# A gated FFN beside a state-space convolution on one core: the convolution as eight block products, a split product in the first two units, one block of LoRA products for the second weight pair, and a last product in two halves

## The chip, the cores and the metric

The kernel runs on one core of a Trainium2 chip. The metric is the device time of one execution in microseconds (us). Five engines work side by side, each with its own instruction queue: TensorE (PE; its weight loads are listed apart as PEld), VectorE (DVE), ScalarE (ACT), GpSimd (POOL) and SyncE (SP), which here only issues DMAs. Matrix products end in PSUM, in banks of 128 rows by 512 f32 columns; the other engines read them from there.

## The reference

The input x has 2 x 1024 tokens of 512 features. Everything is f32. Cut to what is computed:

```python
xn = layernorm(x)                       # over the 512 features, no scale
# s: a state-space (S4) layer along the 512 features of a token
K = s4_kernel(Lambda, p, q, B, Ct, step, 512)   # Cauchy sums at 512 roots of unity, inverse FFT, real part
s = causal_conv(xn, K) + D * xn                  # by FFTs of length 1024, first 512 kept
# g: a SwiGLU FFN with LoRA (rank 16, scale 2) on each of its three weights
h1 = xn @ w1.T + 2 * (xn @ A1.T) @ B1.T          # 512 -> 1376
h3 = xn @ w3.T + 2 * (xn @ A3.T) @ B3.T          # 512 -> 1376
g0 = silu(h1) * h3
g = silu(g0 @ w2.T + 2 * (g0 @ A2.T) @ B2.T)     # 1376 -> 512
out = x + s * g
```

The convolution along 512 features is a product with a 512 x 512 triangular Toeplitz matrix. In blocks of 128 it has only four different blocks, K0 (on the diagonal, with D added) to K3. With a token's features in four blocks X0 to X3, the result has the blocks

Y0 = X0 K0, Y1 = X0 K1 + X1 K0, Y2 = X0 K2 + X1 K1 + X2 K0, Y3 = X0 K3 + X1 K2 + X2 K1 + X3 K0.

## The kernel before

**First stage, to about 270 us.** Features lie on partitions, tokens on columns. The 2048 tokens are four blocks of 512. The products with w1 and w3 are done by two nested levels of a Strassen-Winograd scheme (seven products in place of eight at each level). The hidden features are cut into five pairs of chunks and a last one of 96 rows. A *chain* (`Chain`, `add_chain`) is one sequence of seven inner products; `product` (L745, matmul at L750) issues the matmuls of one, into the banks called x, y, w and aux, of which there are two each. ACT copies bank x when a partial sum is to be kept (`snapshot`, L770), while the next product goes on accumulating into the same bank; DVE adds bank y to the copy (L774). Work that belongs between the matmuls is placed by hand: `at(place, what)` puts a call at a place on a time line counted in products (seven to a chain), `after(delay, what)` at so many places behind the present one.

The LoRA part is merged into the weights before they are used. `lora_product` (matmul at L381) multiplies the two rank-16 factors, which lie in 16 of 128 partitions, and `merge` (DVE, L391) adds the product out of PSUM to the weight tile. There are four groups of partitions (0, 32, 64, 96), and products on different groups run side by side on PE. Factors are loaded by `load_lora` into one group, for a range of hidden features: the first `LSPLIT` of them or the rest, `LSPLIT` to `HID`; the rest belongs to the last chunk and the first pairs, and is in use first. Before the change groups 0 and 1 get the rest at the start (on ACT's queue), groups 2 and 3 the first `LSPLIT` (on SP's queue), and `other_factors` later loads the first `LSPLIT` into groups 0 and 1 too. So the second pair, which needs the rest, has two groups: `merge_pair` does four products on them for one half of the features, at place 5.7, and again for the other half at 8.9. The later pairs have four groups, and `merge_whole_pair` does all eight products at once, into banks y, w and two aux.

The gated hidden values g go out to DRAM (`store_g`, L802, on SP's queue).

**Second stage, 270 us to the end.** The product with w2 is done in eight *units* of 256 tokens (128 from each of two blocks), again by seven products P1 to P7 of one Strassen-Winograd level, in half banks of 256 columns. `unit` (L1293) is a generator, and `run` steps two units, or one alone, in turn; after each step it takes one entry from a list of `parts` and, from step `s4_from` on, `s4_steps` entries from `s4_work`. The parts are mostly the group sums of the next group's g (`group_piece`, DVE, L1158: sums of blocks of a g chunk loaded by `load_g`, L1147). `s4_work` is a generator that computes the convolution's matrix on DVE, with a few matmuls: the resolvent (PE L595, DVE L613 to L627), a product at L639, the roots (DVE L648 to L673), then z, the scaled DFT tables (DVE L688 and L690, eight of each), which PE multiplies at L709, and the matrix itself in `conv`, 128 x 640 (`s4_matrix`, from L695).

The first four units only make g for their tokens and set it aside in DRAM (`set_aside`, L1277), since the matrix isn't there yet. The last four (`HOLD` = 4) do the convolution for their own tokens and for those of one unit that was set aside (`held`), which makes 16 products of 128 tokens each, `conv_product` (L915, matmuls at L922). `result` (L1284) adds what is missing in the convolution (L1288), multiplies it by the gate (L1289), adds x (L1290, on POOL, the last one on DVE) and writes the output. `silu` is L1249; L1326 and L1340 are the additions in a unit that free banks w and y.

In units 0 and 1 (`wait=True`) P1 is done without its last chunk first, and then, a step later, its last chunk, whose g comes in latest by DMA; P2 comes after both.

Before the change a convolution takes seven matmuls, two of them with 256 columns:

```python
m = (X0 + X1) K2                       # into bank w, copied by ACT
y[:, 0:256]   = X0 [K0 K1]
y[:, 256:512] = X2 [K0 K1]             # blocks 2 and 3
y[:, 384:512] += X0 K3'                # K3' = K3 - K2
y[:, 128:256] += X1 K0
y[:, 256:384] += X1 K12                # K12 = K1 - K2
y[:, 384:512] += X3 K0
y[:, 256:512] += [m m]                 # by DVE, L1288
```

The token sums X0 + X1 (`token_sums`, L1418, two DVE operations of 128 x 1024) stand at the head of the parts of units 2 and 3, behind two empty entries and ahead of the group sums of the next group.

The last unit's last product, P3, goes into one half bank of 256 columns and accumulates onto z4's source (bank x, which holds the earlier products); silu, the gate, x and the write follow for 256 columns at once.

Of the kernel before, what the change touches and what calls it, by code (L numbers as in the profile page):

```python
# [12 lines left out]
F32 = mybir.dt.float32  # L13
# [94 lines left out]
def s4_gated_ffn(  # L108
# [308 lines left out]
    def merge_whole_pair(c, w):  # L417

        ps = [[bank("y", True), bank("w", True)], [bank("aux"), bank("aux")]]
# [7 lines left out]
        for (k, v), when in zip(((0, 0), (0, 1), (1, 0), (1, 1)), (1.15, 2.3, 4.3, 4.4)):  # L427
            to = w[:, (slice(1, 3), slice(0, 4, 3))[v], k].rearrange("p s m h -> p s (m h)")
            from_ = ps[k][v].rearrange("p (s n) -> p s n", s=2)
            after(when, lambda to=to, from_=from_: merge(to, from_))  # L430
# [201 lines left out]
    def s4_roots():  # L632
# [50 lines left out]
        for lc in range(NDC):  # L683
            e_r, e_i = edft[:, 0, lc, :], edft[:, 1, lc, :]
            a_r, a_i = ar[:, lc : lc + 1], ai[:, lc : lc + 1]
            for i, (f, g, o) in enumerate(((a_i, a_r, add), (a_r, a_i, sub))):
                tz = s4_tile([P, P], "tz")
# [7 lines left out]
    def s4_matrix():  # L695
# [42 lines left out]
        k1, k2, k3, k12 = (conv[:, n * P : (n + 1) * P] for n in range(1, 5))  # L738
        nc.vector.tensor_tensor(k12, k1, k2, sub)
        yield  # L740
        nc.vector.tensor_tensor(k3, k3, k2, sub)
# [173 lines left out]
    def conv_product(lhs, x01, sb, tok, tag):  # L915

        y, m_ps = bank(tag), bank("w")[:, :P]
        x0, x1, x2, x3 = (lhs[i][:, sb, k, tok] for i in range(2) for k in range(2))
        k = [conv[:, n * P : (n + 1) * P] for n in range(5)]

        def mul(to, x_, by, start=False):
            nc.tensor.matmul(  # L922
                to, lhsT=x_, rhs=by, start=start, stop=True, skip_group_check=True
            )

        mul(m_ps, x01[:, sb, tok], k[2], True)
        m = work.tile([P, P], F32, tag="m", name="m", bufs=3)
        nc.scalar.copy(m, m_ps)
        mul(y[:, : 2 * P], x0, conv[:, : 2 * P], True)
        mul(y[:, 2 * P :], x2, conv[:, : 2 * P])  # L930
        mul(y[:, 3 * P :], x0, k[3])
        mul(y[:, P : 2 * P], x1, k[0])
        mul(y[:, 2 * P : 3 * P], x1, k[4])
        mul(y[:, 3 * P :], x3, k[0])
        return y, m
# [29 lines left out]
    for v, f in enumerate(factors):  # L965
        load_lora(nc.sync, 2 + v, *f, 0, LSPLIT)

    def other_factors():
        for v, (_, h) in enumerate(factors):
            load_lora(nc.sync, v, None, h, 0, LSPLIT)  # L970
# [113 lines left out]
    for c in range(NPAIR):  # L1084
# [7 lines left out]
        if c + 1 < NPAIR:  # L1092
# [8 lines left out]
            if c == 0:  # L1101
                for half in range(2):
                    at(5.7 + 3.2 * half, step(merge_pair, half))
# [147 lines left out]
    class Place:  # L1251
# [21 lines left out]
        def conv(self, h, tag):  # L1273
            return conv_product(lhs[h], x01[h], self.sb, self.tok, tag)
# [9 lines left out]
        def result(self, h, y, cols=slice(0, DIM), last=False):  # L1284
            o, (y, m) = self.o[h][:, cols], y
            if cols.stop == DIM:
                late = y[:, HALF:].rearrange("p (n t) -> p n t", n=2)
                nc.vector.tensor_tensor(late, late, m.unsqueeze(1).broadcast_to([P, 2, P]), add)  # L1288
# [4 lines left out]
    def unit(u, read, held=None, wait=False):  # L1293
# [21 lines left out]
        if wait:  # L1315
            pairs = [t[:, c, cut] for t in a11 for c in range(t.shape[1])]
            pairs = list(zip(pairs, b11))
            product(xb, pairs[:-1], True)
            yield
            product(xb, pairs[-1:], False)  # L1320
# [4 lines left out]
        mul(wb, a12, b21, True, [(gl[:, 0, cut], wl0)])  # L1325
# [17 lines left out]
        if last:  # L1343
# [9 lines left out]
            mul(*p3)  # L1353
            pl.result(1, y[1], lo)
            silu(o0[:, hi], xb)
            pl.result(0, y[0], hi, True)
# [50 lines left out]
    for part in (*s3, *s2):  # L1407
# [4 lines left out]
    run([unit(u, read, wait=True) for u in range(2)], [*t[:2], *s1, *s4_, *t[2:], *more], 4, 5)  # L1412
# [3 lines left out]
    x01 = [work.tile([P, NSB, TB], F32, name=f"x01_{h}", bufs=1) for h in range(2)]  # L1416
    token_sums = [
        lambda h=h: nc.vector.tensor_tensor(  # L1418
            x01[h], lhs[h][0][:, :, 0, :], lhs[h][0][:, :, 1, :], add
        )  # L1420
        for h in range(2)
    ]
# [10 lines left out]
    nothing = [lambda: None]  # L1433
# [97 lines left out]
```

## Time and profile before

| | us |
|---|---|
| median of 3 runs | 447.9 |
| fastest and slowest run | 447.69, 448.11 |
| the profiled execution, its own time | 447.56 |
| its span (first to last instruction) | 445.8 |

The TensorE clock granted in the profiled execution is full speed (1.0) in every slice. Of the 40 slices of the span (11.1 us each), PE is 90% busy or more in all but the first and the last; DVE is at 80% or more from 11 to 89 us, at 30 to 80% with single slices above it until 279 us, at 70 to 100% from there to 334 us, and at 10 to 50% from then on. ACT is busy 137.4 us in all, POOL 202.2.

A line of a timeline is: start in us, length in us, engine, line of the code, operation, output <- inputs, form, number of records (x2 means two records of the same kind one behind another; an f32 matmul leaves more than one record). In square brackets stands the idle time of the engine just before, and what ended it. Matmuls overlap, so the pitch from one start to the next is what a matmul costs, not its length. A line of DMA issues is: output <- input, queue, number, size, microseconds from issue to landing. In the list of waits a line is: engine and line that waited, what for; total, times, longest.

### The profile page before, as it was taken

The page shows a single profiled execution, that of the slowest core. Times are in us where ns is not written, and L with a number is a line of the kernel's source. Part 1 is how long each engine was busy: PE and PEld are TensorE (multiplying, and loading weights), DVE is VectorE, ACT ScalarE, POOL GpSimd, SP SyncE. Part 2 cuts the span into 40 slices and gives each one's busy share as a digit, 9 for nine tenths or more (in the row PEclk, how much of TensorE's full clock was granted, in tenths as well). Part 3 has the DMA queues.
Part 4 walks back from the last instruction along what each step waited for, and adds up shares of the span by engine and source line. Part 5 has one row for each costly group of instructions (what it writes and reads, how often), then busy time and mean ns, then how long its engine had stood idle before and what let it go on. Part 6 is the DMA issues. An engine that isn't in the chain of part 4 may idle for free.

```text
span 445.8 us, 5022 instructions
## 1 busy us (share of the span) xinstructions
PE 438.9 (98%) x1678; PEld 272.2 (61%) x1678; DVE 292.0 (66%) x496; ACT 137.4 (31%) x279; POOL 202.2 (45%) x156
## 2 busy tenths in 40 slices
PE   8999999999999999999999999999999999999996
PEld 8635334344444444444443446888898999989995
DVE  5898999946874687368836887979892214541222
ACT  2776342453245334433443242111102101011110
POOL 1315169895679548944894379200000213221221
PEclk9999999999999999999999999999999999999999
DMA  8911304025002400340054536486803742323211
GB/s 263 361 53 46 118 0 147 24 73 165 25 24 97 140 24 24 112 145 24 24 184 147 165 126 199 143 308 205 330 1 114 282 136 76 120 96 94 94 49 47
DMA packets 35257, 53.52 MB, mean 120 GB/s; under 512 B 4640, under 2 KB 21344, under 8 KB 35104
## 3 DMA queue, kind: packets, MB, share of 16 engines
q1 hardware_dynamic: 35104, 53.07, 36.2%
q8 instruction: 13, 0.21, 0.2%
q10 hardware_dynamic: 128, 0.14, 0.1%
q14 instruction: 12, 0.10, 0.1%
HBM read 33.80 MB, written 19.40 MB: 119 GB/s over the span
## 4 chain that ended last, share of the span: by engine, by line
PE 93%; DMA 2%; DVE 1%; issue 1%; POOL 1%; ACT 0%; POOLq 0%; DVEq 0%; SPq 0%
PE x L750 44%; PE y L750 23%; PE w L750 12%; PE aux L922 6%; PE w L975 2%; DMA room<-g_dram 1%; PE aux L303 1%; PE aux L381 1%; PE y L381 1%; PE w L922 1%; PE y L527 1%; PE aux L709 1%; DMA g_dram<-s 0%; POOL s L831 0%; DVE t_in L1200 0%
## 5 line engine op out<-in xcount | busy, mean ns | idle before, releaser
L1290 POOL TENSOR_TENSOR o<-o,xin 128x512 f32<-128x512 f32 (+1 forms) x17 | 22.5, 1324 | 136.9 <-DVE o L1289 136.9
L831 POOL TENSOR_TENSOR s<-c,s 128x512 f32<-128x512 f32 (+1 forms) x44 | 63.6, 1451 | 16.6 <-ACT c L823 11.5
L770 ACT COPY s<-x 128x512 f32<-128x512 f32 (+1 forms) x54 | 31.6, 586 | 87.8 <-PE x L750 86.5
L750 PE MATMUL x<-t_in,s 128*128 128x512 f32 (+1 forms) x148 | 55.2, 500 | 0.0
L774 DVE TENSOR_TENSOR s<-s,y 128x512 f32<-128x512 f32 (+1 forms) x54 | 36.1, 680 | 17.1 <-PE y L750 10.9
L864 POOL TENSOR_TENSOR s<-ua_three,s 128x512 f32<-128x512 f32 x20 | 32.4, 1619 | 26.9 <-DVE s L774 26.9
L750 PEld LDWEIGHTS x<-t_in,s 128*128 128x128 f32 x148 | 26.8, 190 | 22.8 <-issue 12.5
L864 POOL TENSOR_TENSOR ua_three<-ua_three,s 128x512 f32<-128x512 f32 x20 | 33.0, 1650 | 13.6 <-DVE s L774 13.6
L750 PE MATMUL y<-t_in,s 128*128 128x256 f32 (+1 forms) x108 | 35.9, 459 | 0.0
L1312 ACT COPY z<-x 128x256 f32<-128x256 f32 x24 | 8.8, 372 | 79.9 <-PE x L750 79.9
L864 POOL TENSOR_TENSOR s<-u_three,s 128x512 f32<-128x512 f32 x20 | 28.5, 1425 | 1.8 <-ACT c L823 1.0
L823 ACT ACTIVATE c<-c 128x512 f32<-128x512 f32 x40 | 25.2, 632 | 8.8 <-DVE c L864 8.8
L750 PEld LDWEIGHTS y<-t_in,s 128*128 128x128 f32 x108 | 20.1, 190 | 11.5 <-issue 8.8
L788 ACT COPY w<-x 128x512 f32<-128x512 f32 (+1 forms) x37 | 21.1, 570 | 12.2 <-PE x L750 12.1
L922 PE MATMUL aux<-conv,xr 128*128 128x128 f32 (+1 forms) x128 | 23.2, 314 | 0.0
L1288 DVE TENSOR_TENSOR aux<-aux,m 128x256 f32<-128x256 f32 x16 | 6.9, 431 | 23.1 <-PE aux L922 23.1
L864 POOL TENSOR_TENSOR u_three<-ua_three,u_three 128x512 f32<-128x512 f32 x10 | 12.7, 1272 | 18.3 <-DVE u_three L774 18.3
L750 PE MATMUL x<-t_in,w 128*128 128x512 f32 x40 | 20.8, 603 | 0.0
L750 PE MATMUL x<-xr,w 128*128 128x512 f32 x40 | 20.6, 614 | 0.0
L750 PE MATMUL x<-xt,w 128*128 128x512 f32 x40 | 20.6, 597 | 0.0
L750 PE MATMUL x<-xr,s 128*128 128x512 f32 x40 | 20.5, 613 | 0.0
L750 PE MATMUL x<-xt,s 128*128 128x512 f32 x40 | 20.4, 592 | 0.0
(282 smaller groups left out, 877.2 us busy)
## 6 DMA issues: line engine op xcount, KB each, us to landing
g_dram<-s SPq DMA_DIRECT2D x40, 256.0 KB, 2.1
g<-g_dram SPq DMA_DIRECT2D x10, 512.0 KB, 5.8
xin<-in_x_dram SPq DMA_DIRECT2D x16, 256.0 KB, 2.7
out_dram<-o SPq DMA_DIRECT2D x14, 256.0 KB, 2.0
t_in<-g_dram SPq DMA_DIRECT2D x6, 512.0 KB, 4.2
w<-in_w1T_dram SPq DMA_DIRECT2D x10, 256.0 KB, 4.4
w<-in_w3T_dram SPq DMA_DIRECT2D x10, 256.0 KB, 3.9
s<-in_x_dram SPq DMA_DIRECT2D x8, 256.0 KB, 4.3
```

Source lines behind the costliest of these rows:

```text
L381: nc.tensor.matmul(ps, lhsT=d[:, dc * P : (dc + 1) * P], rhs=h, start=start, stop=True, skip_group_check=True,)
L750: nc.tensor.matmul(ps[:, cols], lhsT=lhsT, rhs=rhs if parts == 1 else rhs[:, cols], start=first and i == 0 and part == 0, stop=i == len(pa ...
L770: nc.scalar.copy(t, self.x)
L774: nc.vector.tensor_tensor(t, t, self.y, add)
L788: nc.scalar.copy(self.w, self.x)
L823: nc.scalar.activation(c, c if src is None else src, AF.Silu)
L831: nc.gpsimd.tensor_tensor(g, act, g, mult)
L864: (nc.vector if o < 20 else nc.gpsimd).tensor_tensor(to, a, b, add)
L922: nc.tensor.matmul(to, lhsT=x_, rhs=by, start=start, stop=True, skip_group_check=True)
L975: nc.tensor.matmul(ps[:, i % 4 * P : (i % 4 + 1) * P], lhsT=ident, rhs=ident, start=first and i == 0, stop=True, skip_group_check=True,)
L1290: (nc.vector if last else nc.gpsimd).tensor_tensor(o, o, self.xin[h][:, cols], add)
L1312: nc.scalar.copy(t, xb)
```

## The change

It has four parts.

1. **Convolution.** Eight products of 128 columns replace the seven. A bank w now gets X1 (K0 + K2), X0 (K1 + K2) and X2 (K0 + K1), side by side. ACT copies these 384 columns into a tile m, and the first 128 of them once more behind. Bank y gets X0 K0, X0 K3, (X0 + X1) (-K2) into block 1, (X1 - X2 - X0) K1 into block 2 and (X3 - X2 - X1) K0 onto block 3. DVE then adds m's columns 0 to 384, and then its columns 128 to 512, to y's blocks 1 to 3, one 128 x 384 addition each. The token sums are made in 128 x 512 operations, five for each of four pairs of tokens and super-block (`block_sums`): those of the first super-block are appended to `s4_work`, the others are entries in the parts of unit `HOLD`. The two old token sums leave the parts of units 2 and 3. X3 is overwritten by its sum; the other sums lie in tiles that are free by then. The matrix part makes K0 + K2, K1 + K2, K0 + K1 and -K2 in place of K12 and K3'.
2. **Units 0 and 1.** The steps are now P1 without its last chunk, P2 without its last chunk, P1's last, P2's last. Two empty entries go into the parts behind the first two, and `s4_from` goes from 5 to 7.
3. **LoRA of the second pair.** `merge_whole_pair` at place 5.7 takes the place of the two `merge_pair`. It is given two banks w in place of y and w, and its own delays for the four merges. For this groups 2 and 3 are loaded with the rest of the factors, `LSPLIT` to `HID` (608 columns), and `other_factors` loads the first `LSPLIT` into all four groups: four DMAs where there were two.
4. **The last unit's P3.** It is done in two halves of 128 columns. The first goes into another bank x, from zero, and DVE adds z4 to it; the second accumulates as before. Each half is followed by its own silu, gate, addition of x and write.

```diff
@@ -414,9 +414,9 @@
...
-    def merge_whole_pair(c, w):
-        ps = [[bank("y", True), bank("w", True)], [bank("aux"), bank("aux")]]
+    def merge_whole_pair(c, w, first=None, delays=(1.15, 2.3, 4.3, 4.4)):
+        ps = [first or [bank("y", True), bank("w", True)], [bank("aux"), bank("aux")]]
         for half in range(2):
...
@@ -424,7 +424,7 @@
...
                     )
-        for (k, v), when in zip(((0, 0), (0, 1), (1, 0), (1, 1)), (1.15, 2.3, 4.3, 4.4)):
+        for (k, v), when in zip(((0, 0), (0, 1), (1, 0), (1, 1)), delays):
             to = w[:, (slice(1, 3), slice(0, 4, 3))[v], k].rearrange("p s m h -> p s (m h)")
...
@@ -684,7 +684,7 @@
...
             for i, (f, g, o) in enumerate(((a_i, a_r, add), (a_r, a_i, sub))):
-                tz = s4_tile([P, P], "tz")
+                tz = conv[:, DIM:]
                 nc.vector.tensor_scalar(tz, e_i, f, None, mul)
...
@@ -735,10 +735,14 @@
...
         yield
-        k1, k2, k3, k12 = (conv[:, n * P : (n + 1) * P] for n in range(1, 5))
-        nc.vector.tensor_tensor(k12, k1, k2, sub)
-        yield
-        nc.vector.tensor_tensor(k3, k3, k2, sub)
+        k0, k1, k2, _, k01 = (conv[:, n * P : (n + 1) * P] for n in range(5))
+        k2s = s4["k2s"]
+        both = conv[:, : 2 * P].rearrange("p (n t) -> p n t", n=2)
+        nc.vector.tensor_tensor(k2s, both, k2.unsqueeze(1).broadcast_to([P, 2, P]), add)
+        yield
+        nc.vector.tensor_tensor(k01, k0, k1, add)
+        yield
+        nc.vector.tensor_scalar(k2, k2, -1.0, None, mult)
         yield
...
@@ -912,27 +916,36 @@
...
-    def conv_product(lhs, x01, sb, tok, tag):
-        y, m_ps = bank(tag), bank("w")[:, :P]
-        x0, x1, x2, x3 = (lhs[i][:, sb, k, tok] for i in range(2) for k in range(2))
-        k = [conv[:, n * P : (n + 1) * P] for n in range(5)]
-        def mul(to, x_, by, start=False):
+    def conv_product(lhs, x01, x12, sb, tok, tag):
+        y, shared = bank(tag), bank("w")
+        x0, x1, x2, x321 = (lhs[i][:, sb, k, tok] for i in range(2) for k in range(2))
+        k0, k1, k2, k3, k01 = (conv[:, n * P : (n + 1) * P] for n in range(5))
+        def mul(to, n, x_, by, start=False):
             nc.tensor.matmul(
-                to, lhsT=x_, rhs=by, start=start, stop=True, skip_group_check=True
+                to[:, n * P : (n + 1) * P],
+                lhsT=x_,
+                rhs=by,
+                start=start,
+                stop=True,
+                skip_group_check=True,
             )
-        mul(m_ps, x01[:, sb, tok], k[2], True)
-        m = work.tile([P, P], F32, tag="m", name="m", bufs=3)
-        nc.scalar.copy(m, m_ps)
-        mul(y[:, : 2 * P], x0, conv[:, : 2 * P], True)
-        mul(y[:, 2 * P :], x2, conv[:, : 2 * P])
-        mul(y[:, 3 * P :], x0, k[3])
-        mul(y[:, P : 2 * P], x1, k[0])
-        mul(y[:, 2 * P : 3 * P], x1, k[4])
-        mul(y[:, 3 * P :], x3, k[0])
-        return y, m
+        mul(shared, 0, x1, s4["k2s"][:, 0], True)
+        mul(shared, 1, x0, s4["k2s"][:, 1])
+        mul(shared, 2, x2, k01)
+        m = work.tile([P, DIM], F32, tag="m", name="m", bufs=2)
+        nc.scalar.copy(m[:, : 3 * P], shared[:, : 3 * P])
+        nc.scalar.copy(m[:, 3 * P :], shared[:, :P])
+        mul(y, 0, x0, k0, True)
+        mul(y, 3, x0, k3)
+        mul(y, 1, x01[sb][:, tok], k2)
+        mul(y, 2, x12[sb][:, tok], k1)
+        mul(y, 3, x321, k0)
+        return [y, m, True]
...
@@ -963,11 +976,12 @@
...
     for v, f in enumerate(factors):
-        load_lora(nc.sync, 2 + v, *f, 0, LSPLIT)
+        load_lora(nc.sync, 2 + v, *f, LSPLIT, HID)
...
         for v, (_, h) in enumerate(factors):
-            load_lora(nc.sync, v, None, h, 0, LSPLIT)
+            for group in (v, 2 + v):
+                load_lora(nc.sync, group, None, h, 0, LSPLIT)
...
@@ -1099,8 +1113,12 @@
...
             if c == 0:
-                for half in range(2):
-                    at(5.7 + 3.2 * half, step(merge_pair, half))
+                at(
+                    5.7,
+                    lambda nx=nx: merge_whole_pair(
+                        nx, w_pair[nx], [bank("w"), bank("w")], (1.6, 2.6, 4.8, 5.8)
+                    ),
+                )
             else:
...
@@ -1271,7 +1289,7 @@
...
         def conv(self, h, tag):
-            return conv_product(lhs[h], x01[h], self.sb, self.tok, tag)
+            return conv_product(lhs[h], x01[h], x12[h], self.sb, self.tok, tag)
...
@@ -1282,10 +1300,12 @@
...
         def result(self, h, y, cols=slice(0, DIM), last=False):
-            o, (y, m) = self.o[h][:, cols], y
-            if cols.stop == DIM:
-                late = y[:, HALF:].rearrange("p (n t) -> p n t", n=2)
-                nc.vector.tensor_tensor(late, late, m.unsqueeze(1).broadcast_to([P, 2, P]), add)
+            o, made = self.o[h][:, cols], y
+            y, m, parts = made
+            if parts:
+                for n in range(2):
+                    nc.vector.tensor_tensor(y[:, P:], y[:, P:], m[:, n * P : (n + 3) * P], add)
+                made[2] = False
             nc.vector.tensor_tensor(o, o, y[:, cols], mult)
...
@@ -1313,16 +1333,23 @@
...
         if wait:
-            pairs = [t[:, c, cut] for t in a11 for c in range(t.shape[1])]
-            pairs = list(zip(pairs, b11))
-            product(xb, pairs[:-1], True)
+            one, two = (
+                list(zip([t[:, c, cut] for t in a for c in range(t.shape[1])], b))
+                for a, b in ((a11, b11), (a12, b21))
+            )
+            product(xb, one[:-1], True)
             yield
-            product(xb, pairs[-1:], False)
+            product(wb, two[:-1] + [(gl[:, 0, cut], wl0)], True)
+            yield
+            product(xb, one[-1:], False)
         else:
...
         yield
-        mul(wb, a12, b21, True, [(gl[:, 0, cut], wl0)])
+        if wait:
+            product(wb, two[-1:], False)
+        else:
+            mul(wb, a12, b21, True, [(gl[:, 0, cut], wl0)])
         nc.vector.tensor_tensor(o0[:, lo], z1, wb, add)
...
@@ -1350,10 +1377,19 @@
...
             yield
-            mul(*p3)
-            pl.result(1, y[1], lo)
-            silu(o0[:, hi], xb)
-            pl.result(0, y[0], hi, True)
+            other = bank("x")[:, :P]
+            chunks = [t[:, c, cut] for t in s4_ for c in range(t.shape[1])]
+            for n, to in enumerate((other, xb[:, P:])):
+                part = slice(n * P, (n + 1) * P)
+                cols = slice(HALF + n * P, HALF + (n + 1) * P)
+                pairs = [(a, b[:, part]) for a, b in (*zip(chunks, b22), (gl[:, 0, cut], wl1))]
+                product(to, pairs, n == 0)
+                if n == 0:
+                    pl.result(1, y[1], lo)
+                    nc.vector.tensor_tensor(o0[:, cols], z4[:, part], to, add)
+                silu(o0[:, cols], to if n else o0[:, cols])
+                pl.result(0, y[0], cols, True)
             return
...
@@ -1409,17 +1445,41 @@
...
     after_, more = following(1)
-    run([unit(u, read, wait=True) for u in range(2)], [*t[:2], *s1, *s4_, *t[2:], *more], 4, 5)
+    nothing = [lambda: None]
+    run([unit(u, read, wait=True) for u in range(2)], [*t[:2], *nothing * 2, *s1, *s4_, *t[2:], *more], 4, 7)
...
     lhs = [[xr[:, 0], xr[:, 1]], [room["b12"], xr[:, 2]]]
-    x01 = [work.tile([P, NSB, TB], F32, name=f"x01_{h}", bufs=1) for h in range(2)]
-    token_sums = [
-        lambda h=h: nc.vector.tensor_tensor(
-            x01[h], lhs[h][0][:, :, 0, :], lhs[h][0][:, :, 1, :], add
-        )
-        for h in range(2)
-    ]
+    x12 = [work.tile([P, TB], F32, name=f"x12_{n}", bufs=1) for n in range(3)]
+    x12 = [x12[:2], [x12[2], flat(t_in[6])[:, 11 * HALF : 13 * HALF]]]
+    s4["k2s"] = flat(t_in[6])[:, 13 * HALF :].rearrange("p (n t) -> p n t", n=2)
+    places = [room["w"][:, n * DIM : (n + 1) * DIM] for n in range(5, 8)] + [room["zi"]]
+    x01 = [places[:2], places[2:]]
+    def block_sums(sb, h):
+        x0, x1, x2, x3 = (lhs[h][i][:, sb, k] for i in range(2) for k in range(2))
+        d = x12[h][sb]
+        return [
+            lambda t=t, op=op: nc.vector.tensor_tensor(*t, op)
+            for t, op in (
+                ((x01[h][sb], x0, x1), add),
+                ((d, x1, x2), sub),
+                ((d, d, x0), sub),
+                ((x3, x3, x2), sub),
+                ((x3, x3, x1), sub),
+            )
+        ]
+    block_sums_ = [block_sums(sb, h) for sb in range(NSB) for h in range(2)]
+    def first_sums():
+        for part in block_sums_[0] + block_sums_[1]:
+            part()
+            yield
+    s4_work = itertools.chain(s4_work, first_sums())
     held = {}
...
@@ -1430,10 +1490,9 @@
...
     hold(HOLD)
-    nothing = [lambda: None]
     run(
         [unit(2, read), unit(3, read)],
-        [*nothing * 2, *token_sums, *more],
+        [*nothing * 2, *more],
         8,
...
@@ -1449,6 +1508,8 @@
...
         more = ()
+        if u == HOLD:
+            more = nothing + [lambda of=of: [part() for part in of] for of in block_sums_[2:]]
         if ahead and j == 1:
...
```

## The prediction

> **What bounds the kernel now.** The page's engine totals (busy time and share of each engine) come first, then its chain of work that ended last; the second fence is the list of what TensorE (PE) waited for (in total, times, longest).
>
> ```profile
> PE 438.9 (98%) x1678; PEld 272.2 (61%) x1678; DVE 292.0 (66%) x496; ACT 137.4 (31%) x279; POOL 202.2 (45%) x156
> ...
> PE 93%; DMA 2%; DVE 1%; issue 1%; POOL 1%; ACT 0%; POOLq 0%; DVEq 0%; SPq 0%
> ```
>
> ```profile
> PE w L975 <- POOL ident masks.py:199: 1.4, 1, 1.4
> PE x L750 <- DMA room<-g_dram: 0.7, 1, 0.7
> PE y L750 <- DVE u_three L774: 0.3, 1, 0.3
> PE y L303 <- ACT xr L314: 0.3, 1, 0.3
> ```
>
> PE is busy for 98% of the span, makes 93% of the chain and waits 2.7 us in all. So a matmul taken out pays in full, unless the engine that feeds PE is close behind. I price the matmuls first and then look for places where the slack is small. Times are those of the trace of before (span 445.8, execution 447.56).
>
> **Convolution.** One convolution on PE, from the timeline (start, length, count of records; two records are one f32 matmul):
>
> ```profile
> 351.39 0.38 PE L922 MATMUL w<-conv,x 128*128 128x128 f32 x2
> 351.61 0.60 PE L922 MATMUL aux<-conv,t_in 128*128 128x256 f32 x2
> 352.05 0.59 PE L922 MATMUL aux<-conv,xr 128*128 128x256 f32 x2
> 352.48 0.83 PE L922 MATMUL aux<-conv,t_in 128*128 128x128 f32 x6
> 353.15 0.39 PE L922 MATMUL aux<-conv,xr 128*128 128x128 f32 x2
> 353.37 2.32 PE L750 MATMUL y<-t_in,s 128*128 128x256 f32 x10
> ```
>
> Read from start to start: a 128-column matmul takes 0.22 (353.15 to 353.37; three in 0.67), a 256-column one 0.43. Now 5 x 0.222 + 2 x 0.433 = 1.98, which is 353.37 - 351.39. Afterwards 8 x 0.222 = 1.78. That is 0.20 less, times 16: **-3.2**. Bounds: 3.0 to 3.4 by the reading of the starts (0.22 or 0.223).
>
> A rule speaks against it. The Trainium skill, "TensorE: Matmul & The Clock Gate", section "Back-to-back issue gap", gives a sustained 81 ns at 128 columns and 131 ns at 512, so a short matmul costs far more per column; an estimate from that page (98 ns at 256 by interpolation) makes the new product 8% dearer, 0.16 us each, +2.5 in all, and the sum below 450.4. The f32 rows here are proportional to columns (0.22, 0.43, 0.86 for 512), so they decide.
>
> What hides the rest: per convolution VectorE (DVE) does two 128x384 additions (0.56 each, halfway between the 0.43 of 128x256 and the 0.69 of 128x512) in place of one of 0.43: +0.69, 11 us in all, in a last stage of 101 us where DVE is busy 31.3. ScalarE (ACT) copies 384 and 128 columns (between 0.63 and 0.85 together) in place of 128 (0.26); it is busy 13.1 there. An aux bank is used again only two convolutions later, 4 us at the least, and DVE then needs 1.8 for each. If that cover went, each convolution would wait up to 0.7.
>
> The new sums are 20 DVE operations of 128x512 at 0.66, the two 1.22 ones at L1418 go, and the matrix part gains one small operation. Counted from the end of the L709 matmuls (332.12), the new blocks are ready at 336.8, three sums at 338.8, the other seven follow the second L1369 (342.70) and end at 347.9. The first convolution (347.25) needs those done by 344.5, the next (351.2) the rest and L1326, which ends at 348.4. The other ten, for the second half of the tokens, end by 354.4 and 359.5, needed at 358.8 and 363.2. So 0, with 3 us of slack at each place.
>
> **LoRA of the second pair.** Two blocks of four products cost 1.06 each (30.70 to 31.76, 34.53 to 35.60). The later pairs' eight products on four row groups take 103.23 to 104.30, 1.07. So the block at 34.53 goes. But the next matmul accumulates into a bank that ACT is copying:
>
> ```profile
> 34.14 0.56 ACT L770 COPY ua_three<-x 128x512 f32<-128x512 f32 x1
> ...
> 34.53 1.13 PE L381 MATMUL aux<-lo_h,lo_d 16*128 16x256 f32 x8
> ...
> 35.60 1.12 PE L750 MATMUL x<-xr,w 128*128 128x512 f32 x2
> ```
>
> It can start at 34.8, not 34.53: **-0.8**. Behind it DVE, busy without a gap from 35.70 to 70.5, gains only 0.28 there and 0.5 more where it waited (0.64 before 71.18); the slack at the products of 62.55 is 0.7, enough for 0.8. At 81.32 PE already waits 0.34 for DVE. Bounds 0.28 to 1.07; I take 0.8. The factors of groups 2 and 3 (now 38 KB) are issued by 20.81 and land within 5.4: 26.2, before 30.70. The four later loads stand in SP's queue ahead of the g store of 37.13, wait for products that end at 31.8, and hold nothing up.
>
> **First units' P2 split, and what DVE meets after it.** PE's wait of 0.69 for the last g chunk (until 274.15) gets ten matmuls (4.3) in front of it and goes. But the S4 chain on DVE hangs on the same load and does not come sooner; at L639 (312.14) its slack is 0.4. More important is a moved wait. In the list of parts two L1418 sums stood ahead of the group sums of L1158; without them the first group sum moves to their place:
>
> ```profile
> 310.58 0.43 SPq L1147 DMA_DIRECT2D t_in<-g_dram  x1
> ...
> 312.41 0.42 DVE L1326 TENSOR_TENSOR o<-z,w 128x256 f32<-128x256 f32 x1 [0.74 <-PE w L750]
> 312.75 1.22 DVE L1418 TENSOR_TENSOR x<-xr 128x1024 f32<-128x1024 f32 x1
> ...
> 318.34 0.96 DVE L1158 TENSOR_TENSOR s<-t_in 128x768 f32<-128x768 f32 x1
> ...
> 330.12 0.35 DVE L690 SCALAR_TENSOR_TENSOR t_in<-room,ai,tz 128x128 f32<-128x128 f32 x1
> ```
>
> ```profile
> t_in<-g_dram SPq DMA_DIRECT2D x1, 512.0 KB, 6.1
> ```
>
> The group sum reads the chunk issued at 310.58, which landed 6.1 later, at 316.7. Before, DVE came to it at 318.34; now at 312.8, so it waits 3.9. Behind it in DVE's queue stand the roots (L648 to L671), then z (L688, L690), and PE's L709 waits for z. Counting on with the old steps: roots from 317.6, the second group sum at 318.6, third 320.4, fourth 322.2, fifth 324.0, z from 325.1 (before 323.28: 3.9 of waiting, less 2.4 for the two sums, plus group sums that now lie ahead of z). Inside z one group sum fewer falls (0.27 saved), so the last z ends at 332.04, before 330.47. PE came to the matmul of that z at 331.0; now 332.2, and L709 ends 1.2 later than 332.12. So the split's 0.69 is lost and **+1.2** comes on top. Bounds: -0.69 (chunk on time) to +3.9 (landing as late as the 8.8 us of the table load at 313.57). I take 1.2, from that chunk's own row.
>
> **Last product in two banks.** PE: 12 x 0.222 in place of 6 x 0.433, +0.07. Behind it now:
>
> ```profile
> 441.78 0.38 ACT L1249 ACTIVATE o<-x 128x256 f32<-128x256 f32 x1 [1.72 <-PE x L750]
> 442.19 0.42 DVE L1289 TENSOR_TENSOR o<-o,aux 128x256 f32<-128x256 f32 x1 [1.34 <-ACT o L1249]
> 442.65 0.42 DVE L1290 TENSOR_TENSOR o<-o,xin 128x256 f32<-128x256 f32 x1
> ```
>
> At half the columns: 0.27 (a 128x128 copy is 0.26) + 0.29 + 0.28 in place of 1.22, -0.38; the last write halves from 128 KB (1.7; 256 KB is 2.0): at most -0.15. DVE, with the y additions before it, ends the first half about when the second needs it. **-0.35**, bounds 0 to -0.5.
>
> **Sum.** -3.2 - 0.8 + 1.2 - 0.35 = -3.15. Execution 447.56 - 3.15 = 444.4; the median of the runs is 447.9, 0.34 above that execution, so 444.7.
>
> **Rivals.**
> - The chunk is there in time: the split pays 0.3 (DVE's slack at L639), the sum is -4.05 to -4.4: 443.7. For it: the first two chunks landed in 4.5 and 4.2. Against: 4.2 after 310.58 is still 314.8, 2 us after DVE asks, and the DMA engines are full from 310 to 320.
> - DVE's backlog eats more: LoRA gives 0.28 only, the chunk lands a further us late: 446.2. For it: PE waits for DVE already at 81.32. Against: each place has its slack counted.
> - Slower: DVE runs the new sums at half speed, as the 128x896 sums of L451 do where GpSimd works beside them (1.08 against 2.15). Then the seven sums after 342.70 end at 352.2, L1326 frees the w bank 1.5 late, and in the next unit the ten sums of 1.3 bring the two own convolutions another 4.5 late: 6 in all, 450.7. Slower than before from 3.2 of such waits on. Against: GpSimd is idle for 68.8 us until 350.73, and then works 1.27 at a time.
> - The change does not do what it says: the eight products are in the program on PE, one for one; no chance beside those above.
>
> **Chances.** Forecast 444.7: 0.6 (its own range 443.9 to 445.5). Chunk in time 443.7: 0.2. More backlog 446.2: 0.14. Slower 450.7: 0.06. The range takes the first three, whose unknowns end near 443.0 and 446.3. 0.2% is 0.9 us, about what a measurement of this kernel can tell from no change: faster than 447.0 has 0.6 + 0.2 + 0.12 = 0.92; 0.02 of the backlog case falls within 0.2%; slower is 0.06.
>
> **What would show it.** A convolution of 1.78 from start to start; eight L381 products in 1.07 near 30.7 and the next pair matmul 0.8 sooner; no PE wait for room<-g_dram; DVE waiting 3 to 4 us for t_in<-g_dram after the first L1326 of units 2 and 3, and PE about 1 us in L709 for DVE; no PE wait at the first four convolutions. Wrong if DVE does not wait there, or if PE waits in front of a convolution.

## The result, and the profile after

The changed kernel takes 445.3 us (median of 6 runs, 444.94 to 446.62); the kernel before, on the same chip, 448.0 (447.22 to 448.61). The ratio is 0.9947, with a 95% interval of 0.9935 to 0.9959: 2.7 us less. Forecast were 444.7 and 3.15 less.

The page's engine totals and its chain of work that ended last, for the changed kernel (the same lines for the kernel before stand at the head of the prediction):

```profile
PE 437.1 (98%) x1722; PEld 271.8 (61%) x1722; DVE 318.0 (72%) x534; ACT 144.6 (33%) x296; POOL 206.1 (46%) x156
...
PE 70%; DVE 18%; DMA 7%; issue 2%; ACT 1%; SPq 1%; DVEq 0%; ACTq 0%
```

The list of what PE waited for in the changed kernel (in total, times, longest):

```profile
PE w L989 <- POOL ident masks.py:199: 1.4, 1, 1.4
PE aux L709 <- DVE room L690: 0.7, 1, 0.7
PE y L754 <- DVE u_three L778: 0.4, 1, 0.4
PE y L303 <- ACT xr L314: 0.3, 1, 0.3
```

PE is still busy for 98%. Its wait for the last g chunk is gone, and a wait inside L709 for VectorE's z has come. VectorE works 26 us more, and the chain now runs through it for 18%.

The two profiled executions differ by 1.6 us of span only (445.8 and 444.2), because they began unlike each other. Each starts with 48 matmuls that do no work of the kernel (L975, now L989), and then the first LoRA product. Windows of PE, first before, then after (columns: the stretch, its length, PE's busy time with the number of matmul records in brackets, the clock column, the DMA share, GB/s):

```profile
4.00:5.00 1.00, 1.00 (x7) 1.00 1.04 286
5.00:6.00 1.00, 1.00 (x11) 1.00 1.07 267
```

```profile
5.00:6.00 1.00, 1.00 (x6) 1.00 1.05 281
6.00:7.00 1.00, 1.00 (x7) 1.00 1.03 375
...
8.00:9.00 1.00, 1.00 (x11) 1.00 1.04 362
```

The clock column shows 1.00 in all of them, but PE goes from 6 or 7 records in a microsecond to 11 at 5 us in the one and after 7 us in the other; the granted-clock record of the two traces begins, at full rate, at 5.0 and at 7.5 us. The first LoRA product so starts at 8.66 before and at 9.82 after, and everything behind it is 1.16 later. This has nothing to do with the change (the last section shows it in every kernel), so the places below are counted from that product. The span is then 437.14 before and 434.38 after: 2.76 less (spans are given to a tenth), which agrees with the medians.

Starts of some PE instructions, in us after the first LoRA product, from the timelines (a place's time less the first column, which is counted from the start of the span); the kernels below the first two are those of the experiments:

| kernel | first LoRA product | the pair's matmul that stood behind the second LoRA block | units begin | L639 | end of L709 | last product but one | end of span |
|---|---|---|---|---|---|---|---|
| before | 8.66 | 26.94 | 261.19 | 303.48 | 323.46 | 427.73 | 437.14 |
| after | 9.82 | 26.07 | 260.76 | 302.55 | 323.83 | 425.00 | 434.38 |
| conv_alone | 9.86 | 26.91 | 261.07 | 303.20 | 323.19 | 424.36 | 434.04 |
| lora_alone | 8.46 | 26.14 | 260.85 | 303.12 | 323.11 | 427.37 | 436.64 |
| p2_alone | 9.86 | 26.91 | 261.13 | 303.11 | 323.20 | 427.46 | 436.84 |
| order_alone | 9.78 | 26.90 | 261.16 | 303.34 | 323.95 | 428.21 | 437.62 |
| sums_back | 8.96 | 26.08 | 260.86 | 302.37 | 322.46 | 423.62 | 433.04 |
| tail_back | 9.49 | 26.06 | 261.05 | 302.81 | 322.90 | 424.06 | 433.41 |
| before_less | 8.80 | 27.04 | 261.12 | 303.28 | 323.26 | 427.53 | 436.90 |
| lora_less | 9.82 | 26.07 | 260.75 | 302.89 | 322.88 | 427.14 | 436.38 |
| s4_sooner | 9.86 | 26.07 | 260.95 | 302.37 | 324.95 | 426.12 | 435.64 |

There is one trace of each kernel, and kernels that are alike up to a place do not reach it at exactly the same time. Before, conv_alone, p2_alone and order_alone are alike up to the units and begin them at 261.07 to 261.19; after, lora_alone, sums_back, tail_back and s4_sooner are alike too and begin them at 260.76 to 261.05. At L639 after, sums_back and tail_back, alike up to there, lie between 302.37 and 302.81. So in these two columns a difference of 0.3 to 0.4 between two single traces shows little by itself. The stretches behind them repeat to 0.01: from L639 to the end of L709 it is 19.98 or 19.99 in the kernels that have neither the split of P2 nor a moved group sum, and 20.09 in p2_alone, sums_back and tail_back, which have the split and the group sums in place (in s4_sooner L639 stands one product earlier); from there to the last product but one it is 104.26 or 104.27 with the old convolution and 101.16 or 101.17 with the new one.

**The convolution.** One of them in the changed kernel:

```profile
372.77 0.61 PE L928 MATMUL w<-t_in,xr 128*128 128x128 f32 x4
373.21 0.39 PE L928 MATMUL w<-conv,xr 128*128 128x128 f32 x2
373.44 0.61 PE L928 MATMUL aux<-conv,xr 128*128 128x128 f32 x4
373.88 0.39 PE L928 MATMUL aux<-conv,room 128*128 128x128 f32 x2
374.11 0.39 PE L928 MATMUL aux<-conv,x 128*128 128x128 f32 x2
374.33 0.39 PE L928 MATMUL aux<-conv,xr 128*128 128x128 f32 x2
374.56 0.38 PE L754 MATMUL x<-t_in,s 128*128 128x256 f32 x1
```

Eight products of 0.22 make 1.79 (374.56 - 372.77), as forecast, and the next product follows without a gap. From the end of L709 to the last product but one it is 104.27 before and 101.17 after, 3.10 less over the 16.

**The moved group sum.** VectorE in the changed kernel:

```profile
312.51 0.42 DVE L1353 TENSOR_TENSOR o<-z,w 128x256 f32<-128x256 f32 x1 [0.19 <-PE w L754]
317.13 0.96 DVE L1176 TENSOR_TENSOR s<-t_in 128x768 f32<-128x768 f32 x1 [4.20 <-DMA t_in<-g_dram]
...
332.02 0.35 DVE L690 SCALAR_TENSOR_TENSOR t_in<-room,ai,conv 128x128 f32<-128x128 f32 x1
```

And PE, which needs z in L709:

```profile
330.68 0.39 PE L709 MATMUL aux<-room 128*128 128x128 f32 x2
331.72 0.49 PE L709 MATMUL aux<-room 128*128 128x128 f32 x2 [0.66 <-DVE room L690]
```

VectorE stands for 4.2 us at a chunk that it needs only later, with the S4 chain behind it, and PE meets the delay: L709 ends 21.28 after L639's start, where it took 19.98 before.

### The profile page after: what moved, and what is told of

It reads as the page before. It is cut to its first block, busy times and chain, and to the rows that moved or that the text cites. A ratio compares the mean times of both kernels' runs of the same rounds, so it can differ in the third digit from the quotient of the medians.

```text
span 444.2 us, 5192 instructions
## 1 busy us (share of the span) xinstructions
PE 437.1 (98%) x1722; PEld 271.8 (61%) x1722; DVE 318.0 (72%) x534; ACT 144.6 (33%) x296; POOL 206.1 (46%) x156
## 4 chain that ended last, share of the span: by engine, by line
PE 70%; DVE 18%; DMA 7%; issue 2%; ACT 1%; SPq 1%; DVEq 0%; ACTq 0%
PE x L754 35%; PE y L754 18%; PE w L754 9%; PE aux L928 4%; PE w L928 2%; DVE xt L327 2%; DVE s L1176 2%; DVE w L439 1%; DMA t_in<-g_dram 1%; DMA g<-g_dram 1%; DMA t_in<-in_x_dram 1%; DMA lo_h<-in_b1T_dram 1%; DMA w<-in_w1T_dram 1%; DVE t_in L341 1%; DVE s L451 1%
## 5 line engine op out<-in xcount | busy, mean ns | idle before, releaser
L774 ACT COPY s<-x 128x512 f32<-128x512 f32 (+1 forms) x54 | 31.6, 586 | 87.0 <-PE x L754 85.6
L868 POOL TENSOR_TENSOR s<-ua_three,s 128x512 f32<-128x512 f32 x20 | 35.9, 1793 | 23.7 <-DVE s L778 23.7
L1307 DVE TENSOR_TENSOR aux<-aux,m 128x384 f32<-128x384 f32 x32 | 18.1, 565 | 15.9 <-PE aux L928 14.3
L754 PE MATMUL y<-xt,s 128*128 128x512 f32 x40 | 20.0, 597 | 0.4 <-DVE u_three L778 0.4
```

Of the source, the lines that this page charges most:

```text
L754: nc.tensor.matmul(ps[:, cols], lhsT=lhsT, rhs=rhs if parts == 1 else rhs[:, cols], start=first and i == 0 and part == 0, stop=i == len(pa ...
L774: nc.scalar.copy(t, self.x)
L868: (nc.vector if o < 20 else nc.gpsimd).tensor_tensor(to, a, b, add)
L1307: nc.vector.tensor_tensor(y[:, P:], y[:, P:], m[:, n * P : (n + 3) * P], add)
```

## The experiments

All times are medians; each was compared with runs of the kernel before on the same chip. The ratio to it, with its 95% interval, is given.

**The group sums back in their old place** (sums_back; the changed kernel with one line edited):

```diff
-        [*nothing * 2, *more],
+        [*nothing * 4, *more],
```

> The changed kernel with two more empty entries ahead of the group sums of units 2 and 3, so that these stand where they stood before the change. Theory (the first group sum, two steps early, makes VectorE wait 4.2 us for its g chunk and so TensorE at L709): no VectorE wait for t_in<-g_dram at the first group sum, no TensorE wait of 0.7 at L709, L709 ends about 1.2 us sooner counted from the unit's start, 0.8 to 1.2 us less in all: about 444.3. Rival (the wait only covers another one, VectorE's backlog ahead of the first convolutions): 445.0 to 445.5, with a new TensorE wait between 333 and 355.

Measured: 444.09 us, ratio 0.992 (0.9907 to 0.9934), 1.2 us below the changed kernel. VectorE takes up the first group sum without waiting:

```profile
316.39 0.16 DVE L655 TENSOR_TENSOR qr<-t,t 128x4 f32<-128x4 f32 x1
316.50 0.96 DVE L1176 TENSOR_TENSOR s<-t_in 128x768 f32<-128x768 f32 x1
```

It works on the roots until then, and no wait at L709 is left in the list. From L639 to the end of L709 it is 20.09, against 21.28: 1.19 less. No new wait comes before the convolutions; the rest of the way is 101.16 to the last product but one, as in the changed kernel. The theory holds. It is ahead of both kernels, and only tail_back below, which differs in the last product alone, is as fast.

**The same order in the kernel before** (order_alone; the same work):

```diff
-        [*nothing * 2, *token_sums, *more],
+        [*nothing * 2, *more, *token_sums],
```

> The kernel before with nothing changed but the order of the parts of units 2 and 3: the two token sums (2.4 us of VectorE) behind the group sums instead of ahead of them. Same work. Theory (a VectorE that asks for the g chunk early stalls the roots and z queued behind it): VectorE waits about 4 us for t_in<-g_dram, TensorE about 1 us inside L709, L709 ends 1.0 to 1.2 us later counted from the first LoRA product, 448.8 to 449.2. Rival (in the changed kernel TensorE only met VectorE there because the other edits had brought TensorE forward by 1.3 us): no wait at L709, 447.8 to 448.2.

Measured: 448.4 us, ratio 1.001 (1.000 to 1.002). VectorE waits here too:

```profile
313.39 0.42 DVE L1326 TENSOR_TENSOR o<-z,w 128x256 f32<-128x256 f32 x1 [0.92 <-PE w L750]
317.22 0.96 DVE L1158 TENSOR_TENSOR s<-t_in 128x768 f32<-128x768 f32 x1 [3.41 <-DMA t_in<-g_dram]
```

L709 ends 0.63 later counted from L639 (20.61 against 19.98). PE's own list has no wait at L709 here; its weight loads wait there for VectorE's L690, 0.3 and 0.2. So the moved wait costs by itself, but half of what it costs in the changed kernel; the expectation of 1.0 to 1.2 fell, and its rival is half right. The row says why: counted from the first LoRA product, VectorE goes on at 307.44 here (317.22 - 9.78) and at 307.31 in the changed kernel (317.13 - 9.82), and L709 ends at 323.95 and 323.83. By these rows the landing of the chunk sets both. PE had come to L639 0.79 sooner in the changed kernel (302.55 against 303.34), and all but 0.12 of that is waited away at L709.

**The convolution alone** (conv_alone; the change's part 1 on the kernel before, with four empty entries ahead of the group sums, so that these stay where they stood):

```diff
...
-        [*nothing * 2, *token_sums, *more],
+        [*nothing * 4, *more],
```

> The kernel before with the eight-product convolution and its sums alone, the group sums left where they stood. Theory: 16 x 0.20 less on TensorE and nothing in front of a convolution, 448.0 - 3.2 = 444.8. Rival (the new VectorE sums and additions cost something somewhere): 445.4 or more, with a TensorE wait for VectorE between 333 and 365.

Measured: 445.18 us, ratio 0.9947 (0.9934 to 0.9960). From the end of L709 to the last product but one 101.17, which is 3.10 less than before, with no VectorE wait of PE on the way. The end is 9.68 after that product, where it is 9.41 before: the last write took 2.0 to land in this trace, and 1.7 in that one. This part alone is as fast as the whole change (445.3).

**The LoRA block alone** (lora_alone; the change's part 3 on the kernel before):

```diff
...
-                for half in range(2):
-                    at(5.7 + 3.2 * half, step(merge_pair, half))
+                at(
+                    5.7,
+                    lambda nx=nx: merge_whole_pair(
+                        nx, w_pair[nx], [bank("w"), bank("w")], (1.6, 2.6, 4.8, 5.8)
+                    ),
+                )
```

> The kernel before with the second pair's LoRA in one block alone. The prediction's theory: 0.8 us less, 447.2, kept to the end of the first stage. Rival (VectorE, busy without a gap behind it, gives back most of it): 0.8 less at 36 us, 0.3 to 0.4 less at 82 us and at 270 us, 447.6 to 447.7.

Measured: 447.6 us, ratio 0.9999 (0.9987 to 1.001), which can't tell 0.3 from nothing; the trace can, followed step by step. The pair's next matmul comes 0.80 sooner (26.14 against 26.94), the units begin 0.34 sooner. Between 69 and 75 us PE falls back from 0.79 to 0.21 ahead, in two steps, of 0.33 and 0.25, each at a weight load that waits for VectorE. The first place before, then both with the LoRA block:

```profile
70.00 0.19 PEld L750 LDWEIGHTS x<-xr,s 128*128 128x128 f32 x1 [0.30 <-DVE ua_one L864]
```

```profile
69.59 0.30 PEld L750 LDWEIGHTS x<-xr,s 128*128 128x128 f32 x2 [0.89 <-DVE ua_one L864]
...
74.20 0.30 PEld L750 LDWEIGHTS y<-xt,s 128*128 128x128 f32 x2 [0.88 <-DVE s L774]
```

At the first VectorE has no gap yet and is itself only 0.21 sooner, and PE had no slack: before, the load comes after 0.30 of idle time, where the others there come after 0.24. At the second the L774 that it waits for (at 73.47) stands behind a long sum. VectorE around that sum, first before, then with the LoRA block:

```profile
71.18 0.69 DVE L774 TENSOR_TENSOR u_three<-u_three,y 128x512 f32<-128x512 f32 x1 [0.64 <-ACT u_three L770]
71.78 2.18 DVE L343 TENSOR_TENSOR t_in<-xr,t_in 128x1536 f32<-128x1536 f32 x1
```

```profile
70.19 0.69 DVE L774 TENSOR_TENSOR u_three<-u_three,y 128x512 f32<-128x512 f32 x1
70.79 2.76 DVE L343 TENSOR_TENSOR t_in<-xr,t_in 128x1536 f32<-128x1536 f32 x1
```

GpSimd beside it, again before and with the block:

```profile
72.31 2.78 POOL L864 TENSOR_TENSOR ua_three<-ua_three,s 128x512 f32<-128x512 f32 x1
```

```profile
71.89 2.79 POOL L864 TENSOR_TENSOR ua_three<-ua_three,s 128x512 f32<-128x512 f32 x1
```

The 0.64 that VectorE waited is saved, as the prediction had it, but the sum behind it takes 0.58 longer: started 0.79 sooner, it ends 0.21 sooner. In both it ends 1.65 after the start of the next GpSimd operation (73.96 - 72.31, 73.55 - 71.89 = 1.66), and in the changed kernel as well (72.08 + 2.76 - 73.19 = 1.65). So its end goes by GpSimd's operations, not by its own start, and GpSimd's string of operations is only 0.2 sooner (72.31 - 8.66 = 63.65, 71.89 - 8.46 = 63.43). The Trainium skill, "GPSIMD Engine Reference", "Key points", says that GpSimd shares its SBUF interfaces with VectorE and contends with VectorE instructions that have two SBUF inputs; this sum has two, and the rows agree.

**Two merges left out** (before_less and lora_less: the kernel before and lora_alone, each without two of VectorE's merges of the second pair).

```diff
-            after(1.6 + v, lambda to=to, v=v: merge(to, ps[v]))
+            if not (c == 1 and half):
+                after(1.6 + v, lambda to=to, v=v: merge(to, ps[v]))
```

```diff
-            after(when, lambda to=to, from_=from_: merge(to, from_))
+            if not (first and k):
+                after(when, lambda to=to, from_=from_: merge(to, from_))
```

> The kernel before, with the two VectorE merges (1.28 us) of the second half's LoRA products of the second pair left out, so that those weights lack that LoRA part. The base for the next run. Theory (VectorE's backlog sets the pace up to 82 us): the TensorE wait of 0.34 for u_three there goes. Rival: it stays. Either way 447.4 to 447.9.

> The second pair's LoRA in one block alone, with two of its four VectorE merges (1.28 us) left out, so that half of that pair's weights lack their LoRA part. Against the run with the same merges left out of the kernel before, counted from the first LoRA product: theory (only VectorE kept the 0.8 us from arriving) 0.7 to 0.85 us less at 82 us and at 270 us. Rival (something other than VectorE, a DMA or the products' own order, holds TensorE): 0.2 to 0.4 less, as without leaving them out.

Measured: 447.55 us, ratio 0.9993 (0.9984 to 1.0002), and 447.02, ratio 0.9985 (0.9975 to 0.9995). Leaving the merges out of the kernel before changes nothing at 82 us: the wait of 0.34 stays, 72.76 after the first LoRA product against 72.66. With the LoRA block it is 72.09: 0.67 less, near the 0.7 to 0.85 of the theory. But at the start of the units only 0.37 is left (261.12 - 260.75), as the rival had it. It goes at 238.6, at another place, where VectorE waits for a load of w2 in lora_less:

```profile
238.62 0.69 DVE L391 SCALAR_TENSOR_TENSOR w_a<-y,w_a 128x512 f32<-128x512 f32 x1 [2.73 <-DMA w_a<-in_w2T_dram]
```

and PE for the bank that this merge frees. So two places take the 0.8 back: VectorE and GpSimd from 69 to 75 us, and what is left over about 0.4 at the load of w2. The other traces have the second place too: seven of the eleven name this load there, and VectorE starts the merge at 228.80 to 229.09 with the LoRA block and at 229.11 to 229.24 without, counted from the first LoRA product.

**The P2 split alone** (p2_alone; the change's part 2 on the kernel before, token sums in their place):

```diff
...
+            product(wb, two[:-1] + [(gl[:, 0, cut], wl0)], True)
+            yield
+            product(xb, one[-1:], False)
...
+            product(wb, two[-1:], False)
...
```

> The kernel before with the split of P2 in units 0 and 1 alone, the token sums in their place. Theory (the wait goes, but VectorE's S4 chain does not come sooner and its slack at L639 is 0.4): 0.9 less at 280 us, 0.3 to 0.5 less from 313 us on, 447.5 to 447.7. Rival: the whole wait is saved, 447.1.

Measured: 447.27 us, ratio 0.9991 (0.9981 to 1.0001). The units' products up to P2 end 1.02 sooner (270.63 against 271.65 at the start of the next product), L639 0.37 sooner, the end of the span 0.30. By the ratio that is 0.4 less, with an interval that reaches to 0.85 less, close to the rival; the traces speak for the theory. Half of the 1.02 goes where PE waits for the addition that frees bank y, which stands in VectorE's queue behind the reciprocals of the S4 chain (L584):

```profile
303.21 1.56 PE L750 MATMUL y<-t_in,t_in 128*128 128x256 f32 x6 [0.23 <-DVE o L1347]
```

Ahead of this wait PE is 1.02 sooner than before, at the next matmuls (304.61) 0.52. Each time is read against a kernel before whose wait for that chunk was 0.69; in conv_alone, which keeps the wait, it is 0.5.

**The last product in one bank again** (tail_back; sums_back with the change's part 4 undone):

```diff
-            other = bank("x")[:, :P]
...
+            mul(*p3)
+            pl.result(1, y[1], lo)
+            silu(o0[:, hi], xb)
+            pl.result(0, y[0], hi, True)
```

> The changed kernel with the two empty entries added and the last unit's last product in one bank again. The prediction's theory: 0.35 us more than with two halves (444.1), 444.4 to 444.5. Rival (two writes of 64 KB land no sooner than one of 128 KB, and TensorE has 0.1 more): no difference, 443.9 to 444.2.

Measured: 444.36 us, ratio 0.9913 (0.9899 to 0.9926), against 444.09; the intervals overlap widely. The median lies between the theory and the rival. In the traces the way from the last product but one to the end is 9.42 with two halves (sums_back) and 9.35 with one (tail_back), so they speak for the rival. What the two halves save on VectorE is paid back in two places. PE takes 0.10 longer for them (2.68 from 437.41 to 440.09 in the changed kernel, with 0.22 for the last matmul; 2.58 before, from 438.99 to 441.57). And the writes: issues, count, size, us to landing, first tail_back, then the changed kernel:

```profile
out_dram<-o SPq DMA_DIRECT2D x4, 128.0 KB, 1.7
```

```profile
out_dram<-o SPq DMA_DIRECT2D x2, 64.0 KB, 2.1
```

The last write alone took 1.7 and 2.0. That this is due to its size is not shown: conv_alone's last write of 128 KB took 2.0 as well. In all, the way is 9.24 to 9.68 in the eight kernels with one bank, and 9.38 to 9.52 in the three with two.

**S4 work one step sooner** (s4_sooner; sums_back with one number changed):

```diff
-    run([unit(u, read, wait=True) for u in range(2)], [*t[:2], *nothing * 2, *s1, *s4_, *t[2:], *more], 4, 7)
+    run([unit(u, read, wait=True) for u in range(2)], [*t[:2], *nothing * 2, *s1, *s4_, *t[2:], *more], 4, 6)
```

> The changed kernel with the two empty entries added and the S4 work of units 0 and 1 begun one step sooner (6 in place of 7). Theory (0.2 to 0.4 of what the split of P2 saves is given back between 303 and 313 us, where TensorE waits for a VectorE that is busy with group sums and the S4 chain in turn): L639 0.2 to 0.3 sooner counted from the start of the units, 443.8 to 444.0 against 444.1. Rival (the group sums, now later, hold TensorE up instead): L639 no sooner, 444.1 to 444.6.

Measured: 446.58 us, ratio 0.9972 (0.9962 to 0.9983): slower than sums_back by 2.5 (by 2.3 in the ratios; the two ran on different chips), more than its rival had. L639 starts no sooner than in sums_back (302.37 in both), though one product less of PE stands ahead of it. PE waits for VectorE's addition that frees bank y, which now stands in VectorE's queue behind the S4 chain; the second of its two waits is the longer one:

```profile
PE y L754 <- DVE o L1367: 2.1, 2, 1.5
```

```profile
298.71 1.76 DVE L584 RECIPROCAL den<-den 128x128 f32<-128x128 f32 x2
300.39 0.36 DVE L1367 TENSOR_TENSOR o<-z,y 128x256 f32<-128x256 f32 x1
...
301.53 1.76 DVE L584 RECIPROCAL den<-den 128x128 f32<-128x128 f32 x2
...
304.74 0.42 DVE L1367 TENSOR_TENSOR o<-z,y 128x256 f32<-128x256 f32 x1
```

```profile
300.81 1.56 PE L754 MATMUL y<-t_in,t_in 128*128 128x256 f32 x6 [0.60 <-DVE o L1367]
...
305.22 1.56 PE L754 MATMUL y<-t_in,t_in 128*128 128x256 f32 x6 [1.55 <-DVE o L1367]
```

So the last of the two steps from 5 to 7 in the change, which looked like bookkeeping, is worth that much; 5 was not run with the split of P2.

## Why the prediction was right, and where its sizes were off

The median of 445.3 lies in the range of 443.9 to 445.5, near its slow end. Measured is after less before, counted from the first LoRA product.

| step | predicted | measured | |
|---|---|---|---|
| 16 convolutions | -3.2 | -3.10 | 1.79 each, nothing in front of one |
| LoRA block | -0.8 | -0.87 behind the block, -0.43 where the units begin | half or more given back |
| units to the end of L709 | +1.2 | +0.80 | split -0.95 up to P2's end, +0.45 given back by L639, +1.3 from there, 1.2 of it the wait |
| last product | -0.35 | -0.03 | no gain |
| sum | -3.15 | -2.76 | |

- The convolution was right in every part: the pitch in proportion to columns, the VectorE additions (0.565 each against 0.56), and no wait of PE for the new sums. The rule of the Trainium skill that spoke against it ("TensorE: Matmul & The Clock Gate", section "Back-to-back issue gap") would have made each one dearer; 1.79 against 1.98 says otherwise, and the measurement decides. The slower rival, in which VectorE sums at half speed hold PE up, did not come: no run shows a VectorE wait of PE before the first convolutions.
- The moved wait was right in place and cause, and nearly in length: VectorE waits 4.2 (forecast 3.9) for the chunk, which is there 5.9 after its issue (311.25 to 317.13; forecast 6.1), and PE waits inside L709. Its cost of +1.2 came as 1.19 against the same kernel without the wait; against the kernel before, which the term was meant for, the stretch is +0.80. The rival with the chunk in time falls. Of the rival with more backlog the first half came, a LoRA gain near 0.28, and the second did not: the chunk was not late.
- That the split's gain is lost at this wait was right for the changed kernel. It does not follow from the split alone, which keeps 0.30 where the sums stand in their place.
- The LoRA term was mis-sized, with the lower bound (0.28) nearer than the value taken: the traces with the block begin the units at 260.89 in the mean (five), those without at 261.14 (four), 0.25 less. The step that failed is "0.5 more where it waited (0.64 before 71.18)": the wait did go, but the sum behind it grew by 0.58 beside GpSimd. And the slack of PE was counted at 62.55 and not at 70.0, where there was none and a third of a microsecond went.
- The tail term was mis-sized: VectorE's and ScalarE's saving was there, the shorter landing of a smaller write (at most -0.15) was not; the last write took 0.3 longer (2.0 against 1.7).
- LoRA and units together were forecast as +0.4 at the end of L709 and are +0.37. That they agree so well is luck: LoRA gave 0.4 less than forecast up to the units, and the units cost 0.4 less. Two of the change's parts, and a wait that the third brought with it, cancel there to a loss; the gain of the change is the convolution's.

## What to carry to other kernels

When work is taken out of a list that is stepped one entry at a time, everything behind it moves forward, also to before its data is there; here VectorE then stood for 4.2 us, with all that was queued behind. Two empty entries gave 1.2 us back here, 0.3% for nothing. A gain ahead of a place that a transfer sets is worth only what that place has left to give: count it where the next transfer, or the next shared engine, ends last.

## What the runs showed of the hardware

PE's start differs from execution to execution of the same instructions. In the eleven profiles of this case the first LoRA product, behind the same 48 matmuls, starts at 8.46 (lora_alone), 8.66, 8.80, 8.96, 9.49, 9.78, 9.82 (twice) and 9.86 us (three times); the granted-clock record of the traces begins at full rate between 4.61 and 7.56 us, in the same order. That is a spread of 1.4 us in the time, a third of a per cent, half of what the change gives. The Trainium skill, "TensorE: Matmul & The Clock Gate", section "What's actually happening", puts the change of rate into a free-running window and gives plus or minus 500 ns for it; here the moments lie 2.9 us apart, so for that figure the measurement decides. The full-rate record is 440.319 us long in five traces and 436.906 in six, with nothing between these two lengths, which are 3.413 apart; that agrees with a window. Counting a trace from the first real product takes it out.

VectorE's sum of 128x1536 beside GpSimd took from 2.16 to 2.76 in the eleven profiles, in each of them until 1.65 or 1.66 after GpSimd's next operation began (a sum of that size took 1.75 at 51.92 in before, with GpSimd idle), and a GpSimd addition of 128x512 took 2.78 at that place, where most take 1.27.
